# A plan of its own for the first batch of a conditioned attention kernel

## The chip, the cores and the metric

The kernel runs on one core of a Trainium2 chip. A core has five engines with an instruction queue each: PE (TensorE, the matrix engine; its weight loads are listed apart as PEld), DVE (VectorE), ACT (ScalarE), POOL (GpSimd, here the issuer of indirect DMAs) and SP (SyncE, here the issuer of all plain DMAs). They meet through semaphores. The metric is the device time of one execution in microseconds; lower is better.

## The reference

`x` is 16 batches of 512 channels by 1024 tokens, `mask` holds 0 or 1 for every token, and `Wq`, `Wo` are 512 x 512. Cut to what matters:

```
q = transpose(x) @ Wq.T;  qh = 8 heads of 64 columns
scores = einsum(qh, qh) / 8
logits = (scores * cmask + (1 - cmask) * NEG) * rmask
ctx = softmax(logits) @ qh
out = x + transpose(ctx @ Wo.T)
```

Queries, keys and values are the same matrix. A masked column gets no weight in an active row. An inactive row has logits that are all zero, so its softmax is the plain mean over all 1024 tokens: all inactive rows of a batch share one result, which follows from the mean of `x` over the tokens. About half the tokens of a batch are active.

## The kernel before, in words

Only active tokens are attended to. `order` ranks the 16 batches by their number of active tokens; `permute(b0, b1)` writes the masks of ranks b0 to b1 in that order into `act16` (a compare, a product of (ranks x 8 x 16) elements, L220, and a reduction, L223, all on DVE); `slots`, `hot` and `index` turn a mask into the rows to fetch; `gather` fetches them with indirect DMAs on POOL. A batch has a width of 512, 528 or 544 slots; the first batch has 512.

For each batch n: `xt` transposes the gathered rows on PE and splits them into two 16-bit parts (`xh` on ACT, L477, and `xl` on DVE, L478). `query(n, e, g)` computes half g of 128 channels, "pair" e (two heads), in 12 matmuls (L547); ACT evicts it (L551), and for the second half DVE multiplies the columns past 384 with a mask `hr` (L554). `qsplit` splits a pair into `hl` (L570 to L572, on DVE), from which four DMAs on SP spread it over the partitions as `xx` (L581 to L584); what reads `xx` waits for these DMAs. `value` transposes a pair and copies it to `v` (L614); `squares` (L593 on ACT or L597 on DVE) and a reduction (L598) give squared norms, of which `peaks`, `top` and `bottom` make `nm`, the bias of the exponentials (L661 to L695).

The means of inactive tokens need row sums of `x` as it lies in memory. `load_half` loads a quarter of the channels and half the tokens (256 KB, L453) for batches 0 and 1, `load_all` (L467) the whole row for later batches; `sum_half` sums it on ACT (L459, `accum_out`). `load` and `split` bring in `Wq` and `Wo`: ACT casts the high half, DVE the low half (L190, `wql`, `wol`).

The main loop goes over batches b. A batch has 4 pairs p, and a pair two calls of `scores` (L773), each of which fills the same four PSUM banks with four tiles of 128 rows; four exponentials on ACT (L788) empty them to `p`, and the next call waits for that. `attend` (L808) multiplies with `v`; `recip_sums`, `recip_rows` and `norm` scale the context; `project` (L931) applies `Wo`, and `scatter` writes rows back. Between the pieces of batch b, the pieces of batch n = b + 1 (xt, query, value) and of the gathers of b + 2 are put in at chosen places: 18 steps `st`, each with two halves.

From batch 1 on these places are a dictionary, `plan[(st, half)]`, and PE runs in the order in which the program is written (`manual_schedule`). In batch 0 the pieces are one list `m`, each piece with an estimated cost, dealt over the steps by shares (L1266 to L1281), and a scheduler with priorities orders PE too. On the other engines that scheduler orders the instructions in all batches. `with self.behind(i)` keeps what follows behind instruction i in this order; `once(dma, i)` makes a DMA wait for i.

Ahead of the loop stands the start of batch 0. Its eight half loads wait on SP until its third transpose (L1118); its eight row sums (L1146) stand on ACT between value(0,0) and value(0,1); then come the first peaks and the casts of `wol` (`shift0` and `wide_rest`, L1148), and only behind the peaks' end the splits of pairs 1 and 2 (L1151).

Of the kernel before, what the change touches and what calls it, by code (L numbers as in the profile page):

```python
# [10 lines left out]
F32 = mybir.dt.float32  # L11
# [36 lines left out]
class Fast:  # L48
# [166 lines left out]
    def permute(self, b0, b1):  # L215

        nc, B, n = self.nc, self.B, b1 - b0
        at, mh = self.placed(b0, b1), self.given16
        each = self.sb([P, n, TB, B], F16, "ch", 2)
        nc.vector.tensor_tensor(each, at.unsqueeze(2).broadcast_to([P, n, TB, B]),  # L220
                                mh.rearrange("p b j -> p j b").unsqueeze(1).broadcast_to([P, n, TB, B]), ALU.mult)
        with nc.allow_low_precision(reason="one of the terms is 0 or 1, the others are 0"):
            nc.vector.tensor_reduce(self.act16[:, b0:b1], each, AX.X, ALU.add)  # L223
# [222 lines left out]
    def load_half(self, b, k, after=None):  # L446

        c, h = k // 2, k % 2
        if k == 0:
            self.source(b)  # L450
        t = self.sb([P, T // 2], F32, *((("xm", 2), ("ub", 3), ("xi", 8), ("xi", 8))[k // 2 if b < 2 else 0]))
        src = self.x_nat[bass.ds(self.st[b]["row"], 1), c * P:(c + 1) * P, h * T // 2:(h + 1) * T // 2].rearrange("o p t -> (o p) t")
        self.once(self.nc.sync.dma_start(out=t, in_=src), after)  # L453
        self.st[b]["xm"].append(t)

    def sum_half(self, b, k):
        s = self.st[b]
        with self.behind(*self.exp):
            self.nc.scalar.activation(s["xm"][k], s["xm"][k], AF.Copy, accum_out=s["ms2"][:, k:k + 1])  # L459

# [580 lines left out]
    def run(self, flag):  # L1041
# [61 lines left out]
        with self.behind(self.st[0]["at"], self.pe):  # L1103
# [23 lines left out]
        def half1(k):  # L1127
            with self.behind(*[self.last_xx] * (k > 2)):
                self.load_half(1, k, self.beat)

        def wide_rest():
            with self.behind(self.last_hl):
                for f in wide:
                    f()

# [28 lines left out]

        def permute():
            with self.behind(self.last_hl):
                self.permute(2, B)

        self.paced = True
        begin = g1[4:] + [(1.5, lambda: None)] + query(0, 3, 0) + value(0, 2) + query(0, 3, 1)  # L1170
        begin += xt(1)[:2] + value(0, 3)
        begin += [(0, apart(self.range_x, 0, c)) for c in range(DC)]
        groups = [(2, 4), (4, 8), (8, 11), (11, B - 2), (B - 2, B)]
        todo, carry = [], []
        if True:
            stack = ExitStack()
            for b in range(B + 1):
                o, n = b - 1, b + 1
                if b == 1:
                    self.spots = True  # L1180
# [20 lines left out]
                if n < B:  # L1201
                    q, x, v = (lambda e, g: query(n, e, g)), xt(n)[2 if b == 0 else 0:], (lambda e: [(0.25, L(self.value, n, e))])
                    tc, tv = ((lambda g, f=f, c=c: [(c, L(f, n, g))]) for f, c in ((self.tail_copy, 0), (self.value_tail, 0.25)))
# [6 lines left out]
                    if b:  # L1210
                        pre = [(0, L(self.active, *g)) for g in new[0]]
                        post = [(0.3, L(self.slots, *g)) for g in new[0]] + [(0, L(self.facts_sums, *g)) for g in new[1]]
# [10 lines left out]
                    else:  # L1223
                        m = sums + x + pk(b, 1)
                        for g in new[0]:
                            m += [(0, permute), (0, L(self.active, *g))]
                        m += q(0, 0) + tp(b, 1) + bt(b, 1) + q(0, 1)
                        for g in new[0]:
                            m += [(0.3, L(self.slots, *g))]
                        m += hot + q(1, 0) + q(1, 1) + tc(0) + v(0) + index + take  # L1230
                        m += rng[:2] + tv(0) + rng[2:] + q(2, 0) + v(1)
                        m += q(2, 1) + pk(n, 0) + tp(n, 0) + q(3, 0) + bt(n, 0)
                        m += q(3, 1) + v(2) + tc(1) + [(0, L(self.means, n))]
                else:
# [10 lines left out]
                if b in (1, 2):  # L1245
                    plan[12, 1] += [(0, L(range_w, " oq"[b], c)) for c in range(DC)]
                if b == 0:
                    m = begin + m
                if b + 2 < B:
# [16 lines left out]
                share = [(0, 0) if i is None else ((0, 0.3), (0.4, 0.4), (1.3, 1.3), (1.2, 1.2))[i] for _, i in S]  # L1266
                unit = sum(c for c, _ in m) / sum(map(sum, share)) if b == 0 else 0
                done, goal, pos = 0.0, 0.0, 0

                def fill(st, half):  # L1270
                    nonlocal done, goal, pos
                    if b:
                        for _, f in plan.get((st, half), []):
                            f()
                        return
                    part, end = share[st][half], st == N - 1 and half == 0
                    goal += part * unit
                    while pos < len(m) and (end or (part and done + m[pos][0] / 2 <= goal)):
                        m[pos][1]()
                        done += m[pos][0]  # L1280
                        pos += 1  # L1281

                for st, (p, i) in enumerate(S):
# [6 lines left out]
                    if i == 0:  # L1290
# [6 lines left out]
                        todo = []  # L1297
                    if b == 0 and p == 0 and i == 2 and self.wide[b] > 512:
                        self.tail_scores(b, 0)

                    for _ in range(1 + (i in (0, 2, 3)) if b < B - 2 else -(-len(self.urgent + self.spare) // (N - st))):
# [158 lines left out]
```

## Time and profile before

| What | Before |
|---|---|
| Time, median of 3 runs | 980.95 us (979.9 to 984.29) |
| The profiled execution's own time | 984.38 us |
| Its span, first to last instruction | 982.7 us |
| PE busy | 939.4 us (96%) |
| DVE busy | 715.4 us (73%) |
| ACT busy | 650.3 us (66%) |
| POOL busy | 310.3 us (32%) |
| Mean granted clock of PE | 0.990 |

The page cuts the span into 40 equal slices and gives each engine's busy share in tenths; views by stretch give busy microseconds, the clock that was granted to PE (1.00 is full) and the share of time that the 16 DMA engines were busy. A line of waits names the engine, tile and line that waited, what released it, the total in microseconds, how often, and the longest. A line of a timeline gives start, duration, engine, line, operation, output and inputs, and in brackets how long the engine had been idle and what released it. Matmuls overlap: twelve of a query half are listed with 0.27 us each but start every 0.11 us.

### The profile page before, as it was taken

How to read it: one execution, taken by the hardware profiler on the slowest of the kernel's cores; microseconds unless marked ns; L12 is line 12 of the kernel's file. 1: busy time of each engine (PE TensorE's matmuls, PEld its weight loads, DVE VectorE, ACT ScalarE, POOL GpSimd, SP SyncE). 2: the span in 40 equal slices, each digit the busy share in tenths (PEclk: the TensorE clock that was granted, in tenths of full speed). 3: DMA queues.
4: the chain of work that ended last, by engine and by line, in shares of the span. 5: the costliest groups of instructions: out<-in, count | busy, mean ns of one | idle time of the engine just before them, and what ended most of it. 6: DMA issues, size and time to landing. Idle time of an engine off the chain costs nothing. (4 is left out here: it accounts for less than half of the span.)

```text
span 982.7 us, 22820 instructions
## 1 busy us (share of the span) xinstructions
PE 939.4 (96%) x8124; PEld 583.5 (59%) x8124; DVE 715.4 (73%) x2425; ACT 650.3 (66%) x1685; POOL 310.3 (32%) x309
## 2 busy tenths in 40 slices
PE   6787999999999999999999999999999999999997
PEld 4444656656666665666666666666666656565543
DVE  7687676777776786877688777777877678785663
ACT  4777666657766676776767678665767667565651
POOL 2201013124151342505234241432515135243452
PEclk9999999999999999999999999999999999999999
DMA  5747455567566577656657777654757747555552
GB/s 165 226 134 200 111 136 174 163 190 218 129 200 187 180 203 201 208 150 197 185 175 222 198 228 222 179 169 136 205 177 237 221 134 210 136 164 171 162 174 99
DMA packets 79145, 176.30 MB, mean 179 GB/s; under 512 B 14545, under 2 KB 22481, under 8 KB 79025
## 3 DMA queue, kind: packets, MB, share of 16 engines
q1 hardware_dynamic: 57968, 107.09, 38.9%
q0 software_dynamic: 21056, 67.68, 21.9%
q8 instruction: 66, 1.08, 0.5%
q14 instruction: 55, 0.44, 0.1%
HBM read 91.36 MB, written 33.91 MB: 127 GB/s over the span
## 5 line engine op out<-in xcount | busy, mean ns | idle before, releaser
L788 ACT ACTIVATE p<-pss,nm 128x528 f32<-128x528 f32 (+2 forms) x512 | 354.4, 703 | 101.1 <-PE pss L773 92.6
L808 PE MATMUL pss<-p,v 128*64 128x264 f32 (+2 forms) x2048 | 244.9, 392 | 0.0
L773 PE MATMUL pss<-xx 128*128 128x118 f16 (+17 forms) x1856 | 215.9, 290 | 7.8 <-ACT p L788 5.2
L1000 POOL DMA_INDIRECT y_out<-xa,idx x68 | 84.4, 1242 | 413.3 <-DVE nq L685 97.5
L808 PEld LDWEIGHTS pss<-p,v 128*64 128x64 f32 x2048 | 142.3, 138 | 88.6 <-issue 8.4
L773 PEld LDWEIGHTS <-xx 128*128 128x128 f16 (+1 forms) x1856 | 103.0, 97 | 91.3 <-issue 36.4
L547 PE MATMUL pm<-xh,wqh 128*128 128x264 f16 (+5 forms) x512 | 142.3, 278 | 2.7 <-DVE rr L867 0.8
L547 PE MATMUL pm<-xh,wql 128*128 128x264 f16 (+5 forms) x512 | 141.5, 276 | 0.0
L547 PE MATMUL pm<-xl,wqh 128*128 128x264 f16 (+5 forms) x512 | 141.5, 276 | 0.0
L422 POOL DMA_INDIRECT xa<-x_in,idx x68 | 75.7, 1113 | 125.9 <-DMA xx<-hl 47.0
L547 PEld LDWEIGHTS <-wqh 128*128 128x128 f16 x1024 | 97.1, 98 | 30.4 <-issue 11.4
L788 ACT ACTIVATION_READ_ACCUMULATOR p<-pss,nm 128x1 f32 x512 | 105.3, 206 | 0.0
L931 PE MATMUL pm<-woh,ch 128*128 128x512 f16 x240 | 91.1, 380 | 0.0
L931 PE MATMUL pm<-woh,cl 128*128 128x512 f16 x240 | 90.9, 379 | 0.0
L931 PE MATMUL pm<-wol,ch 128*128 128x512 f16 x240 | 90.9, 379 | 0.0
L551 ACT ACTIVATE q<-pm 128x264 f32<-128x264 f32 (+5 forms) x128 | 50.9, 398 | 46.9 <-PE pm L547 46.7
L937 DVE SCALAR_TENSOR_TENSOR xa<-pm,xa 128x512 f32<-128x512 f32 x61 | 41.6, 682 | 48.7 <-PE pm L931 48.1
L1000 POOL DMA_INDIRECT y_out<-xi,idx x60 | 64.6, 1077 | 35.7 <-PE pss L719 14.4
L614 ACT COPY v<-pm 128x512 f32<-128x512 f32 x64 | 37.5, 586 | 55.1 <-PE pm L610 54.3
L931 PEld LDWEIGHTS <-ch 128*128 128x128 f16 x480 | 44.9, 98 | 47.5 <-issue 4.1
L422 POOL DMA_INDIRECT xi<-x_in,idx x60 | 59.2, 986 | 22.5 <-issue 15.2
L459 ACT ACTIVATE xm<-xm 128x1024 f32<-128x1024 f32 (+1 forms) x60 | 62.3, 1041 | 3.6 <-DMA xm<-x_nat_in 3.6
(230 smaller groups left out, 1461.8 us busy)
## 6 DMA issues: line engine op xcount, KB each, us to landing
xm<-x_nat_in SPq DMA_DIRECT2D x56, 512.0 KB
xx<-hl SPq DMA_DIRECT2D x208, 136.0 KB
rb<-rd SPq DMA_DIRECT2D x72, 132.0 KB
xx<-hl SPq DMA_DIRECT2D x48, 128.0 KB
pt<-c SPq DMA_DIRECT2D x36, 132.0 KB
pt<-p SPq DMA_DIRECT2D x36, 132.0 KB
rb<-rd SPq DMA_DIRECT2D x32, 136.0 KB
ub<-ud SPq DMA_DIRECT2D x16, 256.0 KB
```

The source lines that it names most:

```text
L422: dma = self.nc.gpsimd.indirect_dma_start(out=tile[:n], out_offset=None, in_=self.x, in_offset=bass.IndirectOffsetOnAxis(ap=idx, axis=0))
L459: self.nc.scalar.activation(s["xm"][k], s["xm"][k], AF.Copy, accum_out=s["ms2"][:, k:k + 1])
L547: self.beat = nc.tensor.matmul(pq, lhsT=w[:, c, e * P:(e + 1) * P], rhs=xx[:, c, cols], start=(k == 0), stop=(k == 3 * DC - 1)).ins
L551: nc.scalar.activation(s["q"][:, e, cols], pq, AF.Copy, scale=1.0 / (SX * SW))
L614: nc.scalar.copy(v, pv)
L773: m = nc.tensor.matmul(flat[:, c0:c1], lhsT=w, rhs=x, start=banks[n] not in banks[:n], stop=banks[n] not in banks[n + 1:])
L788: e = nc.scalar.activation(t, flat[:, at:at + A], AF.Exp, bias=s["nm"][p // 2][:, p % 2 * 2 + k:p % 2 * 2 + k + 1], scale=SCALE, accum_out ...
L808: mm = nc.tensor.matmul(pav[k * DK:(k + 1) * DK, g], lhsT=s["v"][p][:, i, k * DK:(k + 1) * DK], rhs=ps[k, i][:, cols], start=(i == 3), sto ...
L931: mm = nc.tensor.matmul(po[:cols.stop - cols.start], lhsT=a[:, e, cols], rhs=w[:, e, :], start=(e == 0 and k == 0), stop=(e == DC - 1 and ...
L937: return self.nc.vector.scalar_tensor_tensor(x, po, 1.0 / (SX * SW), x, ALU.mult, ALU.add).ins
L1000: dma = self.nc.gpsimd.indirect_dma_start(out=self.out, out_offset=bass.IndirectOffsetOnAxis(ap=idx, axis=0), in_=x, in_offset=None)
```

## The change

Batch 0 gets a `plan` like the other batches, `manual_schedule` now starts at batch 0 rather than batch 1, and the list with costs and shares is gone. Batch 0's eight half loads go to buffers of the tag `p`; the first four are issued right behind the weights, the others and four of batch 1's after the first transpose. Its sums come in two groups, and the split of pair 1 moves ahead of the second group, no longer behind the peaks. For batch 1 the last four halves are summed on DVE. `permute` runs for each group of batches that `slots` takes (2, 4, 3, 3 and 2 of them) rather than once for 14, in a buffer of tag `hl`. The casts of `wol` move from before batch 0's scores to the first four steps of batch 1. The diff, cut to its core:

```
@@ permute
-        each = self.sb([P, n, TB, B], F16, "ch", 2)
+        each = self.sb([P, n, TB, B], F16, "hl", 2)
@@ load_half
-        t = self.sb([P, T // 2], F32, *((("xm", 2), ("ub", 3), ("xi", 8), ("xi", 8))[k // 2 if b < 2 else 0]))
+        t = self.sb([P, C], F32, "p", 12)[:, :T // 2] if b == 0 else \
+            self.sb([P, T // 2], F32, *((("xm", 2), ("ub", 3), ("xi", 8), ("xi", 8))[k // 2]))
@@ sum_half
+            if b == 1 and k > 3:
+                with self.nc.allow_low_precision(reason="float32"):
+                    self.nc.vector.tensor_reduce(s["ms2"][:, k:k + 1], s["xm"][k], AX.X, ALU.add)
+                return
@@ run
         self.warm(13)
+        for i in range(DC):
+            self.load_half(0, i)
         for k in range(3):
             with self.behind(self.pe):
                 self.xt(0, k)
             self.warm(2)
-        for k in range(2 * DC):
-            self.load_half(0, k, self.pe)
+            if k == 0:
+                for i in range(DC, 2 * DC):
+                    self.load_half(0, i, self.pe)
+                for i in range(DC):
+                    self.load_half(1, i, self.pe)
...
-        first += [(0, index1)] + value(0, 0) + g1[:1] + query(0, 1, 1)[:1] + g1[1:2]
-        first += [(0, L(self.sum_half, 0, k)) for k in range(2 * DC)]
-        first += value(0, 1) + query(0, 2, 0) + g1[2:3] + query(0, 2, 1)[:1] + g1[3:4]
-        first += [(0, shift0), (0, wide_rest)]
+        sums0 = [(0, L(self.sum_half, 0, k)) for k in range(2 * DC)]
+        split1 = query(0, 1, 1)[1:]
+        first += [(0, index1)] + sums0[:4] + value(0, 0) + g1[:1] + query(0, 1, 1)[:1] + g1[1:2]
+        first += value(0, 1) + split1 + sums0[4:] + query(0, 2, 0) + g1[2:3] + query(0, 2, 1)[:1] + g1[3:4]
+        first += [(0, shift0)]
...
         with self.behind(self.st[0]["top"]):
-            for _, f in query(0, 1, 1)[1:] + query(0, 2, 1)[1:]:
+            for _, f in query(0, 2, 1)[1:]:
...
-                if b == 1:
+                if b == 0:
                     self.spots = True
                     stack.enter_context(self.tc.manual_schedule(engines={mybir.EngineType.PE}))
...
-                        pre = [(0, L(self.active, *g)) for g in new[0]]
+                        pre = [(0, L(f, *g)) for g in new[0] for f in (self.permute, self.active)]
...
+                        plan = {(0, 0): g1[4:] + query(0, 3, 0) + value(0, 2) + rng0,
+                                (3, 0): query(0, 3, 1) + value(0, 3) + pk(b, 1) + x[:1],
+                                (5, 0): x[1:2], (5, 1): x[2:3],
+                                (7, 0): x[3:] + tp(b, 1) + q(0, 0) + bt(b, 1), (8, 1): pre,
+                                (9, 0): q(0, 1), (9, 1): q(1, 0) + post, (11, 0): hot,
+                                (12, 0): q(1, 1) + tc(0) + v(0) + rng[:2], (12, 1): index, (13, 0): take[:3],
+                                (14, 0): tv(0) + q(2, 0) + rng[2:], (14, 1): v(1) + q(2, 1) + pk(n, 0),
+                                (16, 0): q(3, 0) + tp(n, 0) + take[3:], (16, 1): q(3, 1),
+                                (17, 0): bt(n, 0) + v(2) + tc(1) + [(0, L(self.means, n))]}
...
+                if b == 1:
+                    for c in range(DC):
+                        free.setdefault(c, []).append(L(wide_rest, c))
...
                     for k in range(2 * DC):
-                        free.setdefault(k // 2, []).append(lambda k=k: half1(k))
+                        if k >= DC:
+                            free.setdefault(0, []).append(lambda k=k: half1(k))
                         free.setdefault(3 + k // 2, []).append(L(self.sum_half, 1, k))
```

More of the change, by code (lines that the diff above doesn't have):

```diff
@@ L1127, in half1, with wide_rest @@
         def half1(k):
-            with self.behind(*[self.last_xx] * (k > 2)):
+            with self.behind(self.last_xx):
                 self.load_half(1, k, self.beat)
-        def wide_rest():
+        def wide_rest(c):
             with self.behind(self.last_hl):
-                for f in wide:
-                    f()
+                wide[c]()
         def range_w(name, c):
@@ L1163, in apart @@
             return run
-        def permute():
-            with self.behind(self.last_hl):
-                self.permute(2, B)
         self.paced = True
-        begin = g1[4:] + [(1.5, lambda: None)] + query(0, 3, 0) + value(0, 2) + query(0, 3, 1)
-        begin += xt(1)[:2] + value(0, 3)
-        begin += [(0, apart(self.range_x, 0, c)) for c in range(DC)]
         groups = [(2, 4), (4, 8), (8, 11), (11, B - 2), (B - 2, B)]
@@ L1201, in run @@
                 if n < B:
-                    q, x, v = (lambda e, g: query(n, e, g)), xt(n)[2 if b == 0 else 0:], (lambda e: [(0.25, L(self.value, n, e))])
+                    q, x, v = (lambda e, g: query(n, e, g)), xt(n), (lambda e: [(0.25, L(self.value, n, e))])
                     tc, tv = ((lambda g, f=f, c=c: [(c, L(f, n, g))]) for f, c in ((self.tail_copy, 0), (self.value_tail, 0.25)))
@@ L1223, in run @@
                     else:
[L1224 to L1233, printed above, removed]
+                        pre = [(0, L(f, *g)) for g in new[0] for f in (self.permute, self.active)]
+                        post = [(0.3, L(self.slots, *g)) for g in new[0]]
+                        rng0 = [(0, apart(self.range_x, 0, c)) for c in range(DC)]
+                        plan = {(0, 0): g1[4:] + query(0, 3, 0) + value(0, 2) + rng0,
[7 more added lines that the diff above has]
+                                (17, 0): bt(n, 0) + v(2) + tc(1) + [(0, L(self.means, n))]}
                 else:
@@ L1246, in run @@
                     plan[12, 1] += [(0, L(range_w, " oq"[b], c)) for c in range(DC)]
-                if b == 0:
-                    m = begin + m
+                if b == 1:
+                    for c in range(DC):
+                        free.setdefault(c, []).append(L(wide_rest, c))
                 if b + 2 < B:
@@ L1262, in run @@
                     for k in range(2 * DC):
-                        free.setdefault(k // 2, []).append(lambda k=k: half1(k))
+                        if k >= DC:
+                            free.setdefault(0, []).append(lambda k=k: half1(k))
                         free.setdefault(3 + k // 2, []).append(L(self.sum_half, 1, k))
-                share = [(0, 0) if i is None else ((0, 0.3), (0.4, 0.4), (1.3, 1.3), (1.2, 1.2))[i] for _, i in S]
-                unit = sum(c for c, _ in m) / sum(map(sum, share)) if b == 0 else 0
-                done, goal, pos = 0.0, 0.0, 0
                 def fill(st, half):
[L1271 to L1281, printed above, removed]
+                    for _, f in plan.get((st, half), []):
+                        f()
                 for st, (p, i) in enumerate(S):
@@ L1297, in run @@
                         todo = []
-                    if b == 0 and p == 0 and i == 2 and self.wide[b] > 512:
-                        self.tail_scores(b, 0)
                     for _ in range(1 + (i in (0, 2, 3)) if b < B - 2 else -(-len(self.urgent + self.spare) // (N - st))):
```

## The prediction

> **What bounds the kernel now.** I read the slices of the page first, then busy time by stretch, the waits of PE in the worst stretch, and the timelines of ACT and DVE where those waits begin.
>
> ```profile
> PE   6787999999999999999999999999999999999997
> PEclk9999999999999999999999999999999999999999
> ```
>
> A slice is 24.6 us. PE is at 9 tenths from the fifth slice to the last but one: TensorE bounds the kernel everywhere but in the first four slices and at the very end. The change works inside those four slices. The next view gives the stretch, then the engines' busy time (columns: us, PE, PEld, DVE, ACT, POOL, granted clock, DMA share, GB/s).
>
> ```profile
> 0.00:25.00 25.00, 17.13 (x134) 10.33 (x135) 18.65 (x81) 10.09 (x19) 6.97 (x30) 1.00 0.56 167
> 31.60:108.80 77.20, 61.61 (x472) 35.45 (x472) 52.81 (x181) 52.21 (x144) 7.88 (x11) 0.91 0.57 156
> 200.00:400.00 200.00, 197.96 (x1760) 126.24 (x1759) 147.28 (x486) 137.49 (x354) 67.22 (x64) 1.00 0.64 187
> ```
>
> The stretch 31.6 to 108.8 runs from the first scores of batch 0 to the first query of batch 2. PE is idle there for 15.6 us of 77.2, and its clock is 0.91; in 200 to 400 it is idle for 2.0 us of 200 at a clock of 1.00. What PE waited for in that stretch:
>
> ```profile
> PE pss L773 <- ACT p L788: 5.0, 4, 3.1
> PE pm L610 <- DMA xx<-hl: 3.0, 1, 3.0
> PE pm L670 <- DVE smcol L661: 2.2, 1, 2.2
> PE pm L519 <- DVE xl L478: 2.1, 2, 1.2
> PE pm L680 <- DVE m L673: 1.5, 2, 1.0
> ```
>
> L773 (scores) waits until ACT's exponentials (L788) have emptied the same four banks; L670 waits for the peaks of batch 0. Both start here on ACT:
>
> ```profile
> 16.14 0.60 ACT L477 ACTIVATE xh<-pss 128x512 f16<-128x512 f32 x1 [4.57 <-PE pss L519]
> 27.50 0.61 ACT L459 ACTIVATE xm<-xm 128x512 f32<-128x512 f32 x1
> 33.67 0.62 ACT L593 ACTIVATE tmp<-v 128x512 f32<-128x512 f32 x1
> 37.07 0.69 ACT L788 ACTIVATE p<-pss,nm 128x512 f32<-128x512 f32 x1 [2.78 <-DVE nm L683]
> ```
>
> Eight row sums (L459) run from 27.5 to 33.7, and the squares (L593) that the peaks need stand behind them; so the first exponential is at 37.07, although the scores were issued at 31.64. Ahead of 16.14 ACT is idle for 4.57 us. The clock's price is seen in slices of 4 us:
>
> ```profile
> 44.00:48.00 4.00, 2.57 (x8) 0.57 (x8) 1.62 (x6) 1.98 (x7) 0.00 (x0) 0.64 0.83 221
> 60.00:64.00 4.00, 4.00 (x26) 1.43 (x23) 3.94 (x8) 1.09 (x2) 0.00 (x0) 0.72 0.54 160
> 96.00:100.00 4.00, 3.12 (x20) 2.03 (x21) 1.48 (x5) 1.75 (x3) 0.00 (x0) 0.54 0.63 145
> ```
>
> Each follows an idle piece of PE (3.1 us before 45.43, 1.2 and 1.3 us before 57 and 59, 3.0 us before 95.87). Busy time times (1 - clock), over the six dimmed slices: 0.93 + 0.28 + 0.25 + 1.12 + 1.43 + 1.60 = 5.6 us. So PE's work in the stretch is 61.6 - 5.6 = 56.0 us at full clock, and 77.2 - 56.0 = 21.2 us is the most that any order could win there.
>
> **The change part by part.** Row sums of batch 0: four halves are loaded right behind the weights (SP reached its loads at 7.8 and sat waiting 12.6 us for PE), so four sums, 0.62 us each, fall into ACT's idle 4.57 us ahead of 16.14. If 1 MB more, landing beside the four gathers (11.6 to 16.7), is late, the last sum delays the first xh. The bytes moved from 8 to 16 us would rise from 1.24 MB to 2.3 MB, 286 GB/s; 24 to 28 us shows 308. Cost between 0 and 2.0 us; DVE's xl began 0.64 us after its xh was ready, which covers part: I take 0.4.
>
> The other four sums now stand behind both squares. From 25.65, where the instruction order is still that of before: the second eviction of query half (1,1) no longer waits for a sum, value(0,1) is copied at 28.95 to 29.5, its squares end at 30.05, DVE reduces (0.6 us) to 30.8 and takes the peaks at 31.0; transpose, maximum, broadcast and scale take what 35.39 to 36.87 and its 0.16 show, which gives nm at 32.3. The four sums and two evictions on ACT end at 33.1, so the first exponential is at 33.3, 3.8 us earlier. The peaks' transpose now stands on PE inside query half (2,1) and holds it 0.4 us.
>
> The split of pair 1 (L570 to L572, 1.13 us) was behind the peaks, at 37.4, and its four DMAs were issued at 39.1 to 44.4. It now takes the place on DVE of the four output-weight casts (L190, 0.62 us each, 28.3 to 30.9), and its DMAs go out at 30.3. Those casts move to batch 1's first stages, 2.5 us of DVE: they stand ahead of xl of batch 2, whose PE user comes some 6 us later, behind 3.9 us of attend; I price them at nothing, and at 2.5 if that cover is gone.
>
> Permutations: one of 14 batches costs DVE 0.37 + 3.42 + 2.00 = 5.8 us in this stretch; two batches, between the rows at 128 and 1792 elements, about 1.2. The other twelve come back as 2.0 + 1.6 + 1.6 + 1.2 = 6.4 us in batches 2, 6, 9 and 12. DVE is busy 147 of 200 us there, so this costs nothing, 6.4 if all of it held PE.
>
> Batch 1's last four sums move from ACT (0.62 + 0.19) to DVE: 4 x 0.68 by the nearest row, the reduction of 128x512 (L598). The new wait lies here. DVE works in order, and behind the first two of these sums stands the mask of query half (3,1), behind the fourth the xl of batch 1. Their loads stand on SP's queue behind the pair-2 spread, whose split ends at 35.5; four issues of 0.65 make 38.0. In the trace the second such half, issued near 46.1, was waited for until 51.5. Landing between 2.5 us (the gathers' bound: 14.22 to 16.65) and 5.4 us after its issue puts the second half at 41 to 43.9; I take 42.2.
>
> Now PE's waits in the new order, walked through with durations of the trace (scores 1.57, query half 1.33 to 1.39, four transposes 0.5, attend 3.75; exponentials every 0.67). (a) Pair 0's second scores: PE is done with query half (3,0) and value(0,2) at 35.3; ACT has three exponentials, an eviction, a copy and the fourth exponential until 36.8: 1.6 us. (b) value(0,3) waits for the mask: half (3,1) ends at 39.8 plus 0.4 of transposes, the mask at 43.2: 3.0 us, 1.0 to 5.0 by the landings. (c) Batch 1's first query waits for xl, then the second peaks and pair 2's scores: 0.9 + 0.3 + 0.3 = 1.5. (d) The index of batch 2 waits for the slots' chain on DVE, 5.1 us in the trace from 71.2, while PE has 3.4 us of other work: 1.6. (e) value(1,2) waits for its spread: from the end of query half (2,1), 0.4 + 1.7 of split behind norm's work, 2.5 of issues and 2.5 to land, against 5.3 us of PE work: 1.7. (f) All small ones: 2.0, about the 1.7 us of such in the waits of before. Sum 11.4 us.
>
> Stretch: 56.0 + 11.4 = 67.4 against 77.2, a gain of 9.8. One gap, (b), is of the size that was followed by a dimmed clock; the two slices after 44 cost 0.93 + 0.28 = 1.2, which I take (0 to 5.6). [...]
>
> Sum: 9.8 - 1.2 - 0.4 = 8.2 us. From batch 2's first query PE's order is that of before, so the shift stays. The profiled execution took 984.38 (span 982.7 and 1.7 around it), which gives 976.2; it lay 3.4 above the median 980.95, so for the median I forecast 972.7. What a measurement can tell here is 0.5%, 4.9 us: below 976.0 is faster, above 985.9 slower.
>
> **The rivals.** First, a dimmed clock, which ends on the slower side. PE's order in batch 0 is now fixed by hand, so each late operand stops all behind it; six gaps of 1 to 3 us in 67 us could keep the clock low. With 56.0 us of work and 11.4 of gaps, the stretch equals the old 77.2 at a mean clock of 0.85, and costs 4.9 us more at 0.79: about 986. For it: 1.2 and 1.3 us gaps close together gave 0.72. Against it: the 2.2 us gap before 35.71 gave 1.00. Chance 0.13.
>
> Second, the half sums block DVE. If the fourth xi half lands only 5 us after my time, the mask, the third and fourth splits and xl of batch 1 shift, and PE with them: gain 3, about 978, no change. For it: DMA share of 0.83 at 44 to 52. Against it: four of batch 1's halves are loaded before 25 now. Chance 0.09.
>
> Third, the gain is given back: the permutations or the casts hold PE in later batches, 6.4 + 2.5 us at most; half of that gives 977. Against it: PE's largest waits on DVE after 108.8 are 1.2 us. Chance 0.08.
>
> **How the numbers follow.** The forecast has the other 0.70. With waits of 6 us, no dimming and no delay ahead the gain is 15.2 (965.7); with (b) at 5, 2 more of others and 3 of dimming, 77.2 - 71.4 - 3.0 - 0.4 = 2.4 (978.5). The range takes in the second and third rival: 966 to 980. Faster 0.70; same 0.17, the second and third rival; slower 0.13.
>
> **What would show it.** Right: the first exponential near 33.3; PE idle about 11 us, at a clock of 0.97 or more, from the first scores to batch 2's first query, and that stretch near 68 us; first xh within 0.5 us of 16.14; later batches alike. Wrong: a stretch over 75 us, a clock under 0.9 there, a wait of DVE on xi halves of over 4 us, or new PE waits in batches 2, 6, 9 and 12.

## The result and the profile after

The changed kernel takes 978.52 us (median of 14 runs, 976.32 to 980.7) against 982.83 (979.61 to 987.49) of the kernel before on the same chip: a ratio of 0.9959, 95% interval 0.9944 to 0.9974. By this ratio it is 4.0 us faster (the medians differ by 4.3), where 8.2 were forecast, and inside the 0.5% that the prediction took as its bound. The profiled execution took 980.70 (span 978.9); it is the longest of the 14, 2.2 us above their median. Behind the change's lines the numbers of the code move by 5: the scores are now L778, the exponentials L793, value's transposes L612 and L615, and L462 is the new sum on DVE.

The slices of the page are as before but for the last one:

```profile
PE   6787999999999999999999999999999999999996
...
PEclk9999999999999999999999999999999999999999
```

The busy time by stretch (columns: us, PE, PEld, DVE, ACT, POOL, granted clock, DMA share, GB/s):

```profile
31.60:105.80 74.20, 59.09 (x474) 35.27 (x473) 50.42 (x184) 49.09 (x134) 6.83 (x10) 0.95 0.53 150
```

From the first scores (31.9) to batch 2's first query (106.0, before 109.0) PE is idle for 15.1 us of 74.2, where it was 15.6 of 77.2: the forecast 11.4 did not come. The clock is 0.95, was 0.91. So what was won in this stretch is clock, and the waits have only changed places. What PE waited for from 30 to 110 (total, times, longest):

```profile
PE pm L615 <- DMA xx<-hl: 4.8, 2, 3.0
PE pm L612 <- DVE q L559: 1.8, 1, 1.8
PE pss L778 <- ACT p L793: 1.8, 1, 1.8
PE pss L333 <- DVE oht L279: 1.5, 1, 1.5
PE pss L778 <- DMA xx<-hl: 1.4, 1, 1.4
PE pm L552 <- DVE xl L483: 1.1, 2, 0.9
```

The four waits for exponentials, 5.0 us in all, are one of 1.8, and the peaks' 2.2 are 0.3. In their place stand 6.2 us of waits for spreads (`xx<-hl`, the four DMAs on SP behind a split), of which the kernel before had 3.0. After 110 the longest wait is 1.3 us; before it was 2.4.

The first of them shows on ACT, where the first exponential was forecast at 33.3. The timeline of ACT, and then of PE:

```profile
32.53 0.62 ACT L464 ACTIVATE p<-p 128x512 f32<-128x512 f32 x1
...
35.27 0.69 ACT L793 ACTIVATE p<-pss,nm 128x512 f32<-128x512 f32 x1 [1.93 <-PE pss L778]
```

```profile
34.10 1.13 PE L778 MATMUL pss<-xx 128*128 128x512 f16 x6 [1.40 <-DMA xx<-hl]
...
45.07 0.33 PE L612 MATMUL pm<-ident,q 128*128 128x128 f32 x1 [1.80 <-DVE q L559]
...
82.81 0.36 PE L615 MATMUL pm<-two,xx 128*128 128x64 f16 x7 [1.80 <-DMA xx<-hl]
...
93.76 0.53 PE L615 MATMUL pm<-two,xx 128*128 128x64 f16 x7 [3.00 <-DMA xx<-hl]
```

The last row sum ends at 33.1 as forecast; then ACT waits 1.93 us for the scores, and these wait for pair 0's spread, which lands at 34.1. The other three lines are value(0,3) waiting for the mask, value(1,1) and value(1,2) waiting for their spreads. DVE ahead of the mask (L559):

```profile
42.65 0.69 DVE L462 TENSOR_REDUCE ms<-xi 128x1 f32<-128x512 f32 x1 [3.06 <-DMA xi<-x_nat_in]
44.13 0.69 DVE L462 TENSOR_REDUCE ms<-xi 128x1 f32<-128x512 f32 x1 [0.79 <-DMA xi<-x_nat_in]
44.73 0.28 DVE L559 TENSOR_TENSOR q<-q,hr 128x128 f32<-128x128 f32 x1
```

The mask came at 44.73, forecast 43.2. The four slices of 4 us with a dimmed clock:

```profile
44.00:48.00 4.00, 2.93 (x13) 1.08 (x13) 3.39 (x8) 1.86 (x6) 0.00 (x0) 0.74 0.87 333
48.00:52.00 4.00, 4.00 (x32) 2.53 (x32) 3.84 (x15) 3.39 (x9) 0.00 (x0) 0.83 0.59 140
...
92.00:96.00 4.00, 2.24 (x16) 1.29 (x16) 3.02 (x7) 0.59 (x1) 0.00 (x0) 0.71 0.94 281
96.00:100.00 4.00, 4.00 (x35) 2.51 (x35) 2.86 (x8) 2.75 (x7) 0.00 (x0) 0.86 0.44 102
```

Busy time times (1 - clock) gives 0.76 + 0.68 + 0.65 + 0.56 = 2.65 us; forecast 1.2, before 5.6.

### The profile page after: what moved, and what is told of

It is laid out like the page before. It is cut to its first block, busy times and chain, and to the rows that moved or that the text cites. A ratio compares the mean times of both kernels' runs of the same rounds, so it can differ in the third digit from the quotient of the medians.

```text
span 978.9 us, 22828 instructions
## 1 busy us (share of the span) xinstructions
PE 936.1 (96%) x8124; PEld 582.6 (60%) x8124; DVE 718.3 (73%) x2441; ACT 649.0 (66%) x1677; POOL 306.2 (31%) x309
## 5 line engine op out<-in xcount | busy, mean ns | idle before, releaser
L793 ACT ACTIVATE p<-pss,nm 128x528 f32<-128x528 f32 (+2 forms) x512 | 354.4, 703 | 103.9 <-PE pss L778 98.9
L813 PE MATMUL pss<-p,v 128*64 128x264 f32 (+2 forms) x2048 | 242.4, 389 | 0.0
L778 PE MATMUL pss<-xx 128*128 128x118 f16 (+17 forms) x1856 | 215.6, 290 | 5.0 <-ACT p L793 2.0
L1005 POOL DMA_INDIRECT y_out<-xa,idx x68 | 81.8, 1203 | 415.1 <-DVE nq L690 97.5
L778 PEld LDWEIGHTS <-xx 128*128 128x128 f16 (+1 forms) x1856 | 103.8, 97 | 87.0 <-issue 35.6
L422 POOL DMA_INDIRECT xa<-x_in,idx x68 | 73.6, 1082 | 126.7 <-DMA y_out<-xa,idx 44.1
L793 ACT ACTIVATION_READ_ACCUMULATOR p<-pss,nm 128x1 f32 x512 | 105.2, 205 | 0.0
L936 PE MATMUL pm<-woh,cl 128*128 128x512 f16 x240 | 90.9, 379 | 0.0
L936 PE MATMUL pm<-wol,ch 128*128 128x512 f16 x240 | 90.9, 379 | 0.0
L1005 POOL DMA_INDIRECT y_out<-xi,idx x60 | 65.3, 1089 | 34.6 <-PE pss L724 15.1
L836 ACT COPY c<-pss 128x528 f32<-128x528 f32 (+2 forms) x64 | 38.3, 599 | 41.6 <-PE pss L831 26.6
```

The costliest lines, as they stand in the source:

```text
L422: dma = self.nc.gpsimd.indirect_dma_start(out=tile[:n], out_offset=None, in_=self.x, in_offset=bass.IndirectOffsetOnAxis(ap=idx, axis=0))
L778: m = nc.tensor.matmul(flat[:, c0:c1], lhsT=w, rhs=x, start=banks[n] not in banks[:n], stop=banks[n] not in banks[n + 1:])
L793: e = nc.scalar.activation(t, flat[:, at:at + A], AF.Exp, bias=s["nm"][p // 2][:, p % 2 * 2 + k:p % 2 * 2 + k + 1], scale=SCALE, accum_out ...
L813: mm = nc.tensor.matmul(pav[k * DK:(k + 1) * DK, g], lhsT=s["v"][p][:, i, k * DK:(k + 1) * DK], rhs=ps[k, i][:, cols], start=(i == 3), sto ...
L836: self.context_out = nc.scalar.copy(c[:, :A].rearrange("p (g c) -> p g c", g=2), pav).ins
L936: mm = nc.tensor.matmul(po[:cols.stop - cols.start], lhsT=a[:, e, cols], rhs=w[:, e, :], start=(e == 0 and k == 0), stop=(e == DC - 1 and ...
```

## The experiments

The theory to be tested: the start and the priced waits come as forecast, and the missing half of the gain went into spreads that land late, because gathers and row loads are on the same DMA engines, and into the clock that dims behind those waits. Its rivals: the wait for the mask decides; the permutations give the gain back in later batches; or the fixed plan loses it and the start alone would do. Where an expectation names a theory by a letter, the words beside it say which is meant. The kernels are the changed one with the edit shown, unless said otherwise; ratios are to the kernel before on the same chip (982.83 us for the changed kernel, 980.6 to 981.3 for the others, but 998.41 for e5, e6, e8 and e9, which ran on another chip). Waits and query times come from one execution each, and the executions of one kernel spread over 2.7 to 10.1 us; the last column says how far the profiled one lay above the median of its kernel.

| Kernel | Ratio, 95% interval | Waits of value(1,1) and value(1,2) for spreads, us | Batch 2's first query, us | Profiled execution above median, us |
|---|---|---|---|---|
| after | 0.9959 (0.9944 to 0.9974) | 1.80, 3.00 | 106.0 | 2.2 |
| e1_halves_early | 0.9959 (0.9942 to 0.9976) | 1.61, 3.25 | 104.7 | 0.6 |
| e3_split1_behind_peaks | 0.9953 (0.9936 to 0.9970) | 1.49, 2.83 | 103.2 | 0.7 |
| e4_sums_on_act | 0.9955 (0.9939 to 0.9971) | 1.34, 3.19 | 104.0 | 0.4 |
| e2_gathers_late | 0.9954 (0.9937 to 0.9971) | none, 0.71 + 3.06 | 104.9 | 0.3 |
| e8_small_row_loads | 0.9982 (0.9953 to 1.001) | 0.78, 2.92 | 103.5 | -0.8 |
| e13_gathers_early | 0.9933 (0.9916 to 0.9951) | 1.31, 1.12 | 102.3 | 3.2 |
| e16_value2_alone | 0.9925 (0.9902 to 0.9948) | 1.53, none | 100.1 | 0.9 |
| e5_values_later | 0.9912 (0.9882 to 0.9941) | none | 97.5 | 0.8 |
| e6_values_later_halves_early | 0.9921 (0.9892 to 0.9949) | none | 98.5 | -1.0 |
| e9_halves_early_fill | 0.9946 (0.9914 to 0.9978) | 0.64, 1.38 | 103.9 | 0.7 |
| e14_gathers_held | 0.9979 (0.9965 to 0.9993) | 2.06, 0.62 | 102.8 | -2.1 |
| e10_start_only | 0.9981 (0.9965 to 0.9996) | none, 3.87 | 107.5 | 0.8 |
| e11_one_permutation | 0.9987 (0.9974 to 0.9999) | 0.55, 3.08 | 106.2 | -1.6 |
| e35_split_late_values_later | 0.9914 (0.9898 to 0.9930) | none | 95.9 | -0.9 |
| e17_values_later_gathers_early | 0.9907 (0.9883 to 0.9930) | none | 97.2 | 0.0 |
| e18_all_four | 0.9902 (0.9877 to 0.9926) | 0.17, none | 97.8 | 0.9 |

Put down to this stretch, and taken off the query's time, the last column brings the kernels into nearly the order of their ratios (97.2 for e17, 99.1 for e13, 103.8 for the changed kernel, 107.8 for e11): the way to batch 2's first query is where they differ. Without this, e8 and e14 would look faster than the changed kernel, which their times don't show.

**The wait for the mask, taken away in three ways.** In e1 all eight halves of batch 1 are loaded at the start; in e3 the split of pair 1 goes back behind the peaks; in e4 the four sums go back to ACT.

```
e1:  -  for i in range(DC):               # load_half(1, i, self.pe)
     +  for i in range(2 * DC):           # and half1(k) in the main loop left out
e3:  -  first += value(0, 1) + split1 + sums0[4:] + ...
     +  first += value(0, 1) + sums0[4:] + ...
     -      for _, f in query(0, 2, 1)[1:]:
     +      for _, f in split1 + query(0, 2, 1)[1:]:
e4:  -  if b == 1 and k > 3:              # sum_half: the sum on DVE
     +  if False:
```

> All eight half loads of batch 1 are issued together, after the first transpose, so the last four no longer stand on SP behind the spread of pair 2. Theory A (the lost gain went into late DMA landings; the first of them is DVE standing 3.06 + 0.79 + 0.48 us for the xi halves, with the mask, split 3 and xl of batch 1 behind it): DVE's wait on xi goes to under 0.5 us, PE's wait of value(0,3) on the mask from 1.8 us to under 0.5, the clock stays at 1.00 in 44 to 52, and the time falls by 2 to 4 us against the changed kernel (974.5 to 976.5 at its 978.5). Rival B (the order of the instructions, not the loads, limits: PE would wait for ACT's exponentials instead): the mask wait goes, another of the same length takes its place at pair 1's scores, time within 1 us of the changed kernel.

> Undoes one part: the split of pair 1 goes back behind the peaks, with its four DMAs. Theory A (pair 0's first scores wait 1.4 us for the second half of their spread because pair 1's DMAs follow at once): the wait falls to 0.3 us as in the kernel before, the first exponential is 1.1 us earlier, and what comes later decides: pair 1's scores are not waited for by its spread in either, so time 0 to -1.5 us against the changed kernel. Rival D (the gathers of batch 1 on POOL delay the spread): the wait stays at 1.2 us or more, time the same or up to 2 us longer since DVE's split now stands behind the peaks.

> Undoes one part: batch 1's last four row sums are on ACT again, their loads as late as in the changed kernel. Theory A: DVE no longer stands for the xi halves and value(0,3) waits under 0.5 us for the mask, but ACT now stands for the same loads, 2 to 4 us, ahead of pair 1's exponentials; time between -1 and +2 us against the changed kernel. Rival E (the four reductions themselves overload DVE): DVE's relief alone gives -2 us or more.

All three take the wait of 1.8 us away, and the first attend starts at 46.5 to 46.9 instead of 49.3. None is measurably faster than the changed kernel. What came 2.4 to 2.8 us earlier is not lost in the wait of value(1,2): that is as long as before (2.83 to 3.25 us) and ends at 90.9 to 91.4 instead of 93.8. Part is lost behind it, where the clock dims more deeply (0.79, 0.50 and 0.85 from 88 to 100 in e1: 2.8 us of busy time, 1.7 in e3, 2.2 in e4, 1.2 in the changed kernel). What is left is about what the changed kernel's profiled execution lay above its median. So the wait for the mask is not where the forecast gain went; whether a gain of less than 2 us is in it, these intervals can't tell. In e3 pair 1's own DMAs are out of the way of pair 0's spread, and the first scores wait 2.05 us for it instead of 1.40: these DMAs are not what delays it.

**The spreads of batch 1's values.** e2 puts the gathers of batch 2 behind value(1,1) (from 75.6 us), e13 all of them ahead of both; e8 loads and sums only 64 of the 1024 tokens of batch 2's rows.

```
e2:  -  (13, 0): take[:3], (14, 1): v(1) + q(2, 1) + pk(n, 0), (16, 0): q(3, 0) + tp(n, 0) + take[3:]
     +  (14, 1): v(1) + take + q(2, 1) + pk(n, 0), (16, 0): q(3, 0) + tp(n, 0)
e13: +  (13, 0): take, (14, 1): v(1) + q(2, 1) + pk(n, 0), (16, 0): q(3, 0) + tp(n, 0)
e8:  +  n = 64 if b == 2 else T           # load_all: t[:, :n], x_nat[..., :n]
```

> The gathers of batch 2 are put in behind value(1,1) instead of ahead of it and of query half (3,0). Theory A (value(1,1) waits 1.8 us because its spread shares the DMA engines with three gathers of 256 KB): that wait falls under 0.5 us; the gathers then land on the next spread, so the wait of value(1,2), 3.0 us, stays or grows by up to 1 us; time -2 to 0 us against the changed kernel. Rival C (the spread is late because its split on DVE is late): the wait of value(1,1) stays at 1.5 to 2 us and the time is the same within 0.5 us.

> Leaves out most of the row sums of batch 2: its four loads of 512 KB take 32 KB each, and the sums go over 64 tokens. Everything else as in the changed kernel. Theory G (the DMA engines are full when the spreads are sent, so whatever shares them delays the spreads): the wait of value(1,1), with a 512 KB load in flight at 79.7, falls by 0.5 to 1.5 us; the wait of value(1,2) falls by 0 to 1 us, because gathers and the load for batch 3 remain; first query of batch 2 1 to 3 us earlier. Rival H (a spread takes 4 us from issue to landing however free the engines are): both waits stay within 0.3 us.

> The changed kernel with all five gathers of batch 2 at step 13, none at step 16. If gathers on the same DMA engines delay the spreads, the value(1,1) spread, which then shares with five instead of three, makes PE wait 2.5 to 3 us (1.8 in the changed kernel), and value(1,2) only 1.5 to 2.2 (3.0). Time about the same: ratio to before 0.995 to 0.998. If gathers don't matter, both waits stay within 0.3 us of the changed kernel's.

For value(1,1) e2 tells. PE reached it 5.7 us after the first issue of its spread, as in the changed kernel, and did not wait at all, as expected; no gather was beside this spread (the first came at 82.67 instead of 75.63). In all ten kernels that read it at this place with three or four gathers beside its spread it waited, 0.55 to 2.06 us. How long is less sure: 0.55 came in a kernel that does nothing to it (e11), so the 0.78 of e8 is no proof for the row loads, and in e13, with four gathers instead of three, the wait fell instead of rising to 2.5 to 3. That half of the expectation is wrong. For value(1,2) the wait was 2.83 to 3.25 us in the changed kernel and in the five that leave its place and its gathers alone (e1, e3, e4, e8, e11; e9 puts work ahead of it, and e14 comes below), 3.06 in e2, which has four gathers beside it instead of two, and 1.12 in e13, which has none. PE in e2, and then in e13:

```profile
80.59 0.41 PE L615 MATMUL pm<-two,xx 128*128 128x64 f16 x8
```

```profile
82.58 0.36 PE L615 MATMUL pm<-two,xx 128*128 128x64 f16 x7 [1.31 <-DMA xx<-hl]
...
91.62 0.36 PE L615 MATMUL pm<-two,xx 128*128 128x64 f16 x7 [1.12 <-DMA xx<-hl]
```

The issue of the spread (SP) and the gathers (POOL), in the changed kernel and then in e13:

```profile
87.52 0.47 SPq L586 DMA_DIRECT2D xx<-hl  x1
88.34 0.95 POOL L422 DMA_INDIRECT xa<-x_in,idx  x1 [9.27 <-ACT p L793]
89.60 0.87 POOL L422 DMA_INDIRECT xt<-x_in,idx  x1 [0.30 <-issue]
```

```profile
84.62 0.88 POOL L422 DMA_INDIRECT xt<-x_in,idx  x1 [4.02 <-PE pm L867]
87.29 0.47 SPq L586 DMA_DIRECT2D xx<-hl  x1
```

In e13 the spread landed 4.3 us after its first issue, in the changed kernel 6.2. In e14 the first gather starts 2.05 us behind that issue instead of 0.82, and the spread landed after 4.3 as well. Gathers are not all: in the kernel before and in e10 no gather is beside this spread, but a row load of 512 KB goes out about 1 us ahead of it, and its first reader waited until 6.0 and 6.9 us after the first issue. That is read from the traces; no run takes this row load away.

The clock in e13 stayed at 1.00 from 88 to 104, and of all that keep the values in their place it has the lowest ratio, though its interval overlaps those of the changed kernel, e1 to e4 and e9.

**The values moved behind other work.** e5 puts value(1,1) behind query half (2,1) and carries value(1,2) into batch 1; e6 is e5 with e1; e16 carries value(1,2) alone.

```
e5:  -  (14, 1): v(1) + q(2, 1) + pk(n, 0),
     +  (14, 1): q(2, 1) + v(1) + pk(n, 0),
e5, e16:
     -  (17, 0): bt(n, 0) + v(2) + tc(1) + [(0, L(self.means, n))]}
     +  (17, 0): bt(n, 0) + tc(1) + [(0, L(self.means, n))]}
     +  carry = v(2)
```

> value(1,1) stands behind query half (2,1) instead of ahead of it, and value(1,2) goes into batch 1, behind its query half (0,1); loads, gathers and spreads are as in the changed kernel. Theory A (what ate the gain is that PE reaches these two pieces before their spreads have landed, 1.8 + 3.0 us, and the dimmed clock behind it, 1.2 us): both waits go under 0.5 us, the clock stays at 1.00 in 88 to 104, the first query of batch 2 is at 100 to 102 us instead of 106.0, ratio to the kernel before 0.990 to 0.992. Rival B (the order limits, not the landings): PE then waits for ACT's exponentials or for the gathers of batch 2 by the same 5 us, and the ratio stays at 0.995 to 0.996.

> As the run with the two values later, and with all eight half loads of batch 1 issued together as well. Theory A: both gains add, 4 to 6 us at the values and 2.4 us at the mask of pair 3, first query of batch 2 at 98 to 100 us, ratio 0.987 to 0.990. Rival F (PE is held next by something that both hide, say batch 2's gathers, so the second gain is lost): same as with the values alone, within 1 us.

> The changed kernel with value(1,2) alone carried into batch 1, value(1,1) as it was. If value(1,2) and the dimmed clock behind it carry most of the loss: its 3.0 us wait and the 2.4 us of dimming after 92 us are gone, value(1,1) waits 0.5 to 1.8; batch 2's first query at 99 to 102 instead of 106.0, ratio 0.990 to 0.993. If value(1,1) matters as much, ratio 0.993 to 0.995.

e5 and e16 decide. PE's three largest waits in e5 are those that the prediction had priced; the fourth, 1.3 us for pair 0's spread, it had not, and no value waits for a spread:

```profile
PE pm L612 <- DVE q L559: 1.9, 1, 1.9
PE pss L778 <- ACT p L793: 1.8, 1, 1.8
PE pss L333 <- DVE oht L279: 1.5, 1, 1.5
```

The clock is 1.00 from 40 to 104, the stretch to batch 2's first query lasts 65.7 us (forecast 67.4 without dimming), and the gain is 0.88%, 8.6 us of 980.95, near the forecast of 8.2. That it is so near is in part luck: e5 has neither the 1.7 us that the prediction gave value(1,2) nor its 1.2 of dimming, and pays elsewhere for the moved value, as e16 shows. The wait for the mask is still there, 1.9 us. e16 alone brings the query from 106.0 to 100.1, of which value(1,2)'s wait is 3.0, the 0.6 for ACT ahead of it, the dimming behind it 1.2 and its own eight matmuls 0.7, 5.5 in all. By the ratios e16 wins 3.3 us: some 1.4 us come back in batch 1, where the carried value stands ahead of the first scores (query to scores 4.4 us, 3.0 in the changed kernel). e6 shows that gains don't add: with the mask's wait gone too, its ratio is no better than that of e5, its query comes later (98.5), and the clock was 0.57 from 72 to 76.

**The clock behind a wait.** e9 is e1 with twelve matmuls of 128x512 ahead of value(1,2), whose result nothing reads, to keep PE busy while the spread lands.

```
e9:  +  (17, 0): bt(n, 0) + [(0, L(self.fill_pe, 12))] + v(2) + tc(1) + ...
```

> As the run with the early half loads, and 12 matmuls of 128x512 that nobody reads are put in ahead of value(1,2), where PE waited 3.2 us for the spread and the clock was 0.79, 0.50 and 0.85 in the three slices of 4 us that follow. Theory K (the dimmed clock behind a gap costs time by itself): the wait shrinks by 2.6 us and the clock stays at 0.95 or more, so the first query of batch 2 is 2 to 2.7 us earlier than with the early half loads alone, at about 102. Rival L (the clock dims for another reason, or what follows waits for ACT anyway): that query stays at 104.7 within 0.5 us.

The clock is 1.00 from 88 to 104, where e1 had 0.79, 0.50 and 0.85. From batch 1's query half (3,0) to the attend behind it e9 takes 10.9 us (85.2 to 96.1), e1 13.3 (83.4 to 96.7), although PE has more to do. The 2.4 us are the clock's price of this wait, for waits and filling work take 4.4 to 4.5 us in both. Its ratio is not clear of e1's: at its first scores the profiled execution waited 4.2 us for pair 0's spread, so its query comes late all the same.

**The parts of the change.** e10 is the kernel before with the new start alone (early halves, sums in two groups, split of pair 1 ahead, DVE sums, casts later; no plan, one permutation). e11 is the changed kernel with the one permutation of 14 batches back in batch 0.

```
e11: -  pre = [(0, L(f, *g)) for g in new[0] for f in (self.permute, self.active)]        # b == 0
     +  pre = [(0, L(self.permute, 2, B))] + [(0, L(self.active, *g)) for g in new[0]]
```

> The changed kernel's start (early half loads of batch 0, its sums in two groups, the split of pair 1 ahead, batch 1's last sums on DVE, casts later), with batch 0's main loop ordered as before (the list with costs, PE scheduled too) and the single permutation. If the fixed plan is what loses the forecast gain (its order leaves too little time between a spread's DMAs and the value that reads it), the start alone gives as much as the whole change: ratio to before 0.993 to 0.997, first exponential near 33 to 35. If the plan gives the gain and the start little, the ratio is 0.998 to 1.002. If both give part, each about 2 us: 0.998.

> The changed kernel with the one permutation of 14 batches back in batch 0: 5.8 us of DVE there instead of 1.2, and none in batches 2, 6, 9 and 12. By the third rival of the prediction (later permutations hold PE) this would win 2 to 6 us: ratio to before 0.990 to 0.994. By the theory of late spreads nothing is won after batch 2, and in batch 0 the 4.6 us of DVE stand ahead of the slots and of the splits of batch 1: 0 to 4 us lost, ratio 0.996 to 1.000, with the wait for the index (1.5 us) up to 3 to 5.

The start gives about 1.9 us, the plan and the permutations the other 2.1; the intervals of e10 and the changed kernel overlap, so this split is rough. In e10, whose order the scheduler makes, value(1,2) waits 3.87 us, so the late spread is not the fixed plan's doing. e11, which also puts the permutation's product back into tag `ch`, is slower than the changed kernel by about 2.7 us and not faster: the third rival falls. The trace shows what costs it time: the permutation holds DVE for 3.37 us from 50.42 and for 2.00 from 54.48, PE waits 2.35 and 1.40 us for the xl of batch 1 behind it (the changed kernel 0.9 at most), and the clock is 0.61 from 56 to 60. The query at 106.2, as in the changed kernel, is no contradiction: the one profiled execution lay 1.6 us under its median, the other 2.2 above.

**Pair 0's spread.** In e14 the second to fifth gather of batch 1 wait until that spread has landed.

```
e14: +  self.once(dma, held)              # rows: held is the last DMA of pair 0's spread, for b == 1 and j > 0
```

> The changed kernel, in which the second to fifth gather of batch 1 wait until the spread of pair 0 has landed. If these gathers, at 28.4 and 30.8 us, delay that spread: it lands near 32 to 32.7 instead of 34.1, the wait of 1.4 is 0 to 0.4, the first exponential at 33.3 to 34 instead of 35.3; the mask still waits for xi, so the gain at the end is 0 to 1.5 us, ratio to before 0.994 to 0.996. If the spread takes its 3.7 us anyway, the wait stays at 1.2 to 1.6 and the first exponential at 35.

ACT in e14:

```profile
32.70 0.69 ACT L796 ACTIVATE p<-pss,nm 128x512 f32<-128x512 f32 x1 [0.37 <-PE pss L781]
```

The scores wait for no spread, and the exponential starts 2.6 us earlier than in the changed kernel (1.0 of which is an earlier start of all). The held gather starts at 31.89, so the spread had landed by then, at most 2.6 us after its last issue ended (29.34); in the changed kernel it was 3.7 (30.36 to 34.10), with gathers at 28.43, 30.83 and 32.79. So gathers beside a spread delay it by over 1 us here, and by 1.9 in e13. In the kernel before, the gather at 28.39 was held up for 3.39 us on POOL, the next came only at 32.08, and the scores at 31.64 waited for nothing: the row loads that the change moved away seem to have kept the gathers from the spread. That is read from the two traces; no run tested it. How gathers that are issued later than a spread (here at 30.83 and 32.79, its last DMA issued at 29.75) come to delay it, no run shows; measured are the later landings beside gathers, 6.2 us against 4.3 (e13) and 3.7 against at most 2.6 (e14).

The end gained nothing, though: the ratio is 0.9979. What came earlier waited for the mask, 2.67 us instead of 1.80, the clock behind it was 0.81, 0.50 and 0.84 from 40 to 52, and value(1,1) waited 2.06. Even so this execution, the shortest of its 12, has batch 2's first query at 102.8; what the others lost no profile shows.

**Together.** e35 is e3 with e5; e17 is e35 with e13; e18 is e17 with e14.

> The changed kernel with value(1,1) behind query half (2,1) and value(1,2) carried into batch 1, and the split of pair 1 back behind the peaks. Each alone gave 0.9912 and 0.9953. The theory of late spreads: the waits of PE for value's spread are gone, the wait for the mask too, the clock stays at 1.00 to 104 us: ratio 0.987 to 0.991, batch 2's first query at 94 to 97.5. If the mask's wait was hidden anyway by the next one: 0.991 to 0.993, the query at 97.5 to 99.

> The kernel with split of pair 1 late and both values later, and in addition all gathers of batch 2 at step 13. No value waits for its spread there, so the gathers' place should matter no more: ratio 0.990 to 0.992, as without it. If gathers delay scores or values of batch 1 still, 0.987 to 0.990.

> As the one before, and the gathers of batch 1 held until the spread of pair 0 has landed. If that spread's wait (1.7 us with the split late) goes and nothing takes its place: 1 to 2 us less than the one before, ratio 0.988 to 0.990, batch 2's first query at 94 to 95. If the exponentials or the transposes of batch 1 take its place: the same ratio as the one before within 0.001.

PE in e35, from 30 to 110:

```profile
PE pss L778 <- ACT p L793: 1.8, 1, 1.8
PE pss L778 <- DMA xx<-hl: 1.7, 1, 1.7
PE pss L333 <- DVE oht L279: 1.5, 1, 1.5
```

e35 takes 971.56 us (before 980.86), and by the ratios 4.4 less than the changed kernel: it beats both. Its stretch of 64.3 us has 55.5 of work at a clock of 1.00; with the 0.7 of value(1,2), which now stand behind the stretch, that is the 56.0 that the prediction had worked out. Against e5 it wins nothing in time (0.9914 and 0.9912), though the wait for the mask is gone. The gathers' place matters no more (e17), and with pair 0's spread freed the next wait is 3.1 us of PE behind the row means on DVE (e18, the query at 97.8 and not at 94 to 95). The five kernels without late values (e5, e6, e35, e17, e18) lie between 0.990 and 0.992, and their intervals overlap; which of them is best is not settled.

## Where the prediction held and where it failed

Of 8.2 us, 4.0 came. The step that failed is the landing of spreads: (e), sized 1.7 us, measured 3.6, and two more such waits, at value(1,1) and at pair 0's first scores, which the prediction put at nothing. Behind them the clock cost more than forecast. Term by term:

- Start of batch 0: right. First xh at 16.23 (forecast within 0.5 of 16.14; 0.1 us of delay, priced 0.4), `nm` at 32.51 (32.3), the last sum at 33.1 (33.1).
- First exponential: 35.27 for 33.3. The step moved batch 0's 2 MB of row loads from 20 to 25 us to an earlier place and did not ask what they had held back. It seems to have been batch 1's gathers, which now run beside pair 0's spread and, as e14 shows, delay it: 1.4 us on PE, 1.9 on ACT, unpriced.
- (a) 1.8 for 1.6; (c) 1.1 and 0.7 for 1.5; (d) 1.5 for 1.6: right. The four DMAs of pair 1 that the prediction saw at 39.1 to 44.4 are eight, of pairs 1 and 2; no term hangs on it.
- (b) 0.84 for ACT and 1.80 for the mask, 2.6 for 3.0. The size is right, but DVE stood 4.3 us at the four halves (3.06 + 0.79 + 0.48), more than the 4 us that the prediction had named as a sign of being wrong, and the first two halves landed at 42.65 and 44.13. The second rival did not come all the same: the second half was 1.9 us behind its forecast and the fourth was there by 46.51, without a wait, so none was 5 us late; and e1, e3 and e4 take the wait for the mask away and gain nothing that can be measured.
- (e) is the step that failed: 0.6 + 3.0 = 3.6 for 1.7 (its own terms add up to 1.8). From the end of query half (2,1) of batch 1 at 84.57 the split took 3.1 us (forecast 2.1), and the spread landed 6.1 after it (forecast 5.0: 2.5 of issues and 2.5 to land), while PE reached the value 5.4 us after that end, 0.5 of it a small wait (forecast 5.3). The 2.5 us to land came from a gather of batch 0 at a DMA share of 0.73 (14.22 to 16.65); here the share was 0.88 from 88.5 to 94, and the spread landed 3.8 us after the issue of its last DMA. A row of before shows the same spread waited for with 3.0 us. That it has the same size now is in part luck, for then a row load went ahead of it, and now two gathers go beside it.
- value(1,1), 1.8 us, was not listed: its spread is sent at 75.08 to 78.6, beside three gathers (75.63 to 79.1) and ahead of a row load of 512 KB, at a DMA share of 0.98 from 80 to 83. Without the gathers the wait is gone (e2).
- Sum of the waits: 15.1 for 11.4. The terms for spreads are 5.1 over (1.4 + 1.8 + 1.9), the others 1.4 under.
- Clock: 2.65 for 1.2, half of it behind value(1,2). Rival one stayed away: the mean was 0.95, not 0.85.
- Casts and permutations later: 1.1 us of waits for xl after 110, 0.2 before and 0.4 in e11, so less than 1 us where nothing was forecast, and far from the third rival's 8.9.

Stretch, forecast 67.4 + 1.2, measured 74.1: of the difference of 5.5 us 3.7 are waits, 1.4 clock, and the rest is PE work. These are of one execution; e5, e17, e18 and e35, which take the late values away, are clear of the changed kernel in time.

## What to carry to other kernels

When PE's order is fixed, price each operand that comes by DMA with its landing time at the load of that moment: list what else is queued on the DMA engines between its issue and its use, gathers on other queues too (here a spread landed 6.2 us after its first issue with two gathers beside it, and 4.3 after it in e13, without them). A wait that the kernel before already shows (here 3.0 us for the same spread) is a better first guess than the landing time of another transfer, but ask what else was under way beside it then and what will be now. Put independent work between a spread and its reader: that won measurable time here (e5, e35), while shortening what stands ahead won none, neither with the late values (e1, e3, e4) nor without them (e35 against e5). And judge by the times: a single profiled execution lay up to 3.2 us off the median of its kernel here.

## What was not expected of the hardware

The clock dimmed after single waits shorter than the 2.23 us that had left it at 1.00 in the kernel before. In e6 PE stood 1.50 us ahead of 71.32, and the clock was 0.57 from 72 to 76; the same wait of 1.50 left 1.00 in the changed kernel. In e14 PE stood 2.06 us and got 0.50 from 84 to 86, while 1.80 in the changed kernel at the same place left 1.00. It also did so at one wait and not at another of about the same size and place: at the mask 0.84 + 1.80 us gave 0.74 in the changed kernel, 0.84 + 1.88 gave 1.00 in e5. What decides it these traces don't show: they are of different kernels, with one execution each. The clock's price behind a wait was 0 after 1.80 us in the changed kernel and 2.8 us after 3.25 in e1, and none of these traces tells it ahead.
